# Causal scores on two halves of the PE array's rows, both chains' rotary queries in one step, a new order table, and unused products in three of PE's gaps

## The chip, the cores and the metric

The kernel runs on one core of a Trainium2 chip. Its time is the device time of one execution in microseconds (us); where several executions were timed, the median is given. A profile describes one execution: its *span* runs from the first to the last instruction, and a little time lies around it. The engines are PE (TensorE, matrix products), DVE (VectorE), ACT (ScalarE), POOL (GpSimd) and SP (SyncE, which here only issues transfers, DMAs). PE writes its products to PSUM, in banks of 128 rows by 512 values.

## The reference

One block of a perceiver with a routed feed-forward part, on 256 tokens of width 512, in float32:

```
x = x + cross_attention(layernorm(x), context of 25088 tokens)    # sigmoid scores, no softmax
x = x + causal_attention(layernorm(x))                            # 16 heads of 32, rotary part of 32
x = x + experts(layernorm(x))                                     # argmax over 8 experts, relu(g)^2 * u
```

In the causal attention a score is the sum of two products, one over the 32 values of a head and one over 32 rotary values that all heads share:

```
scores = einsum('bqhd,bkhd->bhqk', q, k) + einsum('bqr,bkr->bqk', q_rope, k_rope)[:, None]
scores = where(causal, -inf, scores / sqrt(HD + D_R))
attn   = einsum('bhqk,bkhd->bqhd', softmax(scores), v) @ W_o
```

## The kernel before

Some 490 us of the span go to the cross attention: 49 pieces of 512 context tokens are loaded, split into high and low parts for products in a faster format, and accumulated in two PSUM banks. Nothing of that is touched.

What follows works on the 256 tokens as two *chains* of 128 tokens, `tt` 0 and 1, which run interleaved. Each piece of work is a *step*, a function such as `Sp(tt, u)`, and the last letter tells its engine: `p` PE, `v` and `w` DVE, `a` ACT, `g` POOL, `s` SP; a step ending in `c` is a copy whose engine is its last argument. The table `ORDER` (line 37) names each step once, with its arguments. The steps are recorded in that order, and `in_order` (line 65) ties each instruction to the one before it on its engine, so each engine works strictly in the order of the table and waits when an input is not there. PSUM banks come from a pool of six (`bank`, line 108) that are handed on when their last reader is done.

The steps of a chain, in order of the data:

- `N1v`, `N1g`, `N1w`, `Xp`, `Xc` (lines 455 to 474): sum, layernorm (the root on POOL), transposition to `xT`.
- `CKp`, `CKc`, `KRp`, `KRv`, `Kp`, `VSp`, `VSc`: compressed keys, rotary keys, keys and values. `Qp` and `QRp`: queries (four steps) and rotary queries. A `prod` is four float32 products over 128 rows.
- `Kc`, `KRc`, `Qc`, `QRc` copy these to the operands of the scores. `kbd` (line 338) is block-diagonal: for each group of four heads it has 128 rows, with keys of one head where its rows are and zeros elsewhere, so that one product with all 128 rows gives two heads. It and the queries `qs` are filled with zeros by POOL first.
- `Sp`, `Sv`, `Sa` (lines 566 to 593): the scores of one unit fill one bank: four heads by 128 keys in chain 0 (4 units), two heads by 256 keys in chain 1 (8 units). A product of the bf16 identity with the mask adds minus infinity above the diagonal. `Sv` takes the maximum, `Sa` the exponential with its sum, one instruction for each head.
- `PTp`, `PTc`, `PVp` (lines 596 to 616): the weights are transposed, copied, and multiplied with the values; each head's result takes 32 rows of PSUM, so heads with different rows can share the PE array.
- `R1v`, `R2p`, `R2c`, `ATv`, `ATa`, `ATw`, `WOp`: division by the sums and output product.
- `N2v`, `N2g`, `N2w`, `Yp`, `Yc` (lines 659 to 684): sum, layernorm and transposition for the experts.
- `LGp`, `LGv`, `RKp`, `RKv`, `RPv` (lines 696 to 750): the choice of expert, counts, and the permutation that sorts tokens into 32-row slots of experts. `RWv` and `RWs` read the numbers of three more experts and load their weights (`mg`, `mh`); `RDs` loads their down weights (`md`).
- `GAp`, `GAc`, `GUp`, `GEa`, `GEv`, `ITp`, `ITc`, `DNp`, `DNa`, `DNv`, `SCp`, `OUv`, `OUs`: sorting, expert products, sorting back, output.

Of the kernel before, what the change touches and what calls it, by code (L numbers as in the profile page):

```python
# [20 lines left out]
P = 128  # L21
# [16 lines left out]
EXa ZSv ZSp O1:0:a AV:0 ZRv O2p:0 AV:1 O2a:0 AV:2 O2v:0 AV:3 Vp:0:0 Vp:0:1 Vp:0:2 Vp:0:3 AV:4 N1v:0 AV:5 AV:6  # L38
AV:7 N1g:0 N1w:0 O1:1:a Xp:0 O2p:1 Xc:0:a O2a:1 CKp:0 O2v:1 Qp:0:0 CKc:0:v Kp:0:0 Kp:0:1 Kc:0:0:3:a Kc:0:0:1:v
Vp:1:0 Kc:0:1:1:a Kc:0:1:3:v Vp:1:1 Vp:1:2 Vp:1:3 VSp:0 WOs N1v:1 Qp:0:1 VSc:0:a Qp:0:2 N1g:1 Qp:0:3 N1w:1 Xp:1  # L40
Qc:0:0:a Qc:0:1:v KRp:0 QRp:0 Xc:1:a KRv:0 QRp:1 KRc:0:1:0:v KRc:0:0:0:a QRv:0 Kc:0:1:2:a CKp:1 Kc:0:0:2:a
KRc:0:0:1:v QRc:0:0:v QRc:0:1:a Qp:1:0 Kc:0:0:0:a QRv:1 CKc:1:a KRc:0:1:1:v Kp:1:0 QRc:1:1:v QRc:1:0:a Kp:1:1
Kc:0:1:0:a Sp:0:1 Sp:0:3 Kc:1:0:3:a Sv:0:1 Sa:0:1 Sp:0:2 Sv:0:3 Kc:1:1:3:v Qp:1:1 Sa:0:3 Kc:1:1:1:v Sv:0:2
Qp:1:2 PTp:0:3 PTp:0:1 Sa:0:2 PTc:0:3:v Qp:1:3 PTc:0:1:v PVp:0:3 Qc:1:0:a Qc:1:1:v PVp:0:1 KRp:1 PTp:0:2 KRv:1
Sp:0:0 PTc:0:2:a KRc:1:1:0:v KRc:1:1:1:v Kc:1:1:2:a VSp:1 KRc:1:0:1:v Kc:1:1:0:a Kc:1:0:1:a Sv:0:0 Sp:1:4
Kc:1:0:0:a VSc:1:a KRc:1:0:0:v Kc:1:0:2:v Sa:0:0 Sp:1:6 Sv:1:4 Sp:1:2 Sv:1:6 Sa:1:4 R1v:0 PTp:0:0 Sp:1:1 Sv:1:2
Sa:1:6 PTc:0:0:v R2p:0 Sv:1:1 PTp:1:6 R2c:0:a Sp:1:7 Sa:1:2 Sp:1:5 Sv:1:7 PTp:1:2 Sv:1:5 Sp:1:3 Sa:1:7 PVp:0:2
Sv:1:3 PVp:0:0 PTc:1:6:a PTp:1:7 ATv:0 PTc:1:2:a PTp:1:4 Sa:1:5 PVp:1:6 PVp:1:2 PTc:1:4:v Sp:1:0 ATa:0 PTc:1:7:v
Sa:1:1 PTp:1:5 ATw:0 PVp:1:4 Sa:1:3 PVp:1:7 Sv:1:0 WOp:0:0 PTc:1:5:v WOp:0:1 PTp:1:3 PTp:1:1 PTc:1:3:a WOp:0:2
# [29 lines left out]
def body(ctx, tc, a, out, nch=NCH):  # L79
# [258 lines left out]
    kbd = [sb.tile([P, 2, 4, T], F32, tag="rT", name=f"kbd{i}", bufs=2) for i in range(2)]  # L338
    for i in range(2):
        nc.gpsimd.memset(kbd[i], 0.0)  # L340
# [14 lines left out]
    trig = sb.tile([64, T], F32, tag="qp0", name="trig")  # L355
    nc.sync.dma_start(trig, a["trig"])
    vs = [sb.tile([P, D], F32, tag=f"kp{i}", name=f"vs{i}", bufs=2) for i in range(2)]
    qs = sb.tile([P, 2, 2, KD, P], F32, tag="N0", name="qs", bufs=2)
    nc.gpsimd.memset(qs, 0.0)
# [140 lines left out]
    @step  # L500
    def QRp(tt):
        ps_["qr", tt] = bank(f"qr_ps{tt}")[0:64, 0:P]
        prod(ps_["qr", tt], tt, lambda j: pw["wqr"][:, 64 * j:64 * (j + 1)])

    @step
    def QRv(tt):
        qr[tt] = sb.tile([32, P], F32, name=f"qr{tt}")
        rotated("q", qr[tt], ps_["qr", tt], tt)

    @step  # L510
    def QRc(tt, i, eng):
        r = 64 - 64 * i
        scaled(eng, qs[r:r + 32, tt, i], qr[tt][:, None, :].broadcast_to([32, KD, P]), 0.125)
# [49 lines left out]
    pr, pt, sc, mx = {}, {}, {}, {}  # L563

    def heads(tt, u):
        return (u, 0, 4) if tt == 0 else (u // 2, 2 * (u % 2), 2)

    @step
    def Sp(tt, u):
        g, h0, n = heads(tt, u)  # L570
        nk = P * (tt + 1)
        p3 = sc[tt, u] = bank(f"s{tt}_{u}").rearrange("p (h k) -> p h k", h=n)
        if tt == 0:
            mm(p3, lhsT=identb, rhs=mask[:, None, :].broadcast_to([P, n, P]), start=True, stop=False)
        for h in range(h0, h0 + n, 2):
            mm(p3[:, h - h0:h - h0 + 2, :], lhsT=qs[:, tt, h // 2, g, :], rhs=kbd[g // 2][:, g % 2, h:h + 2, :nk],  # L576
               start=tt == 1, stop=tt == 0 and h == 2)
        if tt == 1:
            mm(p3[:, :, P:], lhsT=identb, rhs=mask[:, None, :].broadcast_to([P, n, P]), start=False, stop=True)

    @step
    def Sv(tt, u):
        mx[tt, u] = sm.tile([P, 4], F32, tag="mx", name=f"mx{tt}_{u}", bufs=4)
        nc.vector.tensor_reduce(mx[tt, u][:, :heads(tt, u)[2]], sc[tt, u], AX.X, ALU.max, negate=True)

    @step
    def Sa(tt, u):
        g, h0, n = heads(tt, u)
# [353 lines left out]
```

## Time and profile before

| What | us |
|---|---|
| median of three runs | 581.35 (580.42 to 581.46) |
| the profiled execution | 580.47 |
| its span | 578.50 |
| last product of the cross attention ends | 490.4 |
| first scores of the causal attention (chain 0) start | 507.32 |
| output product of chain 0 complete, `N2v` starts | 535.40 |
| transposition for the experts, chain 0, starts (`Yp:0`) | 539.56 |
| the same for chain 1 (`Yp:1`) | 546.23 |
| first expert product starts (`GUp:0:0:0`) | 553.08 |
| last product ends | 574.76 |

How to read such numbers: the share of busy time is an average, and matmul ends are modelled, so a full PE row does not tell that PE could not go faster. The granted clock tells how fast the array was allowed to run; it is shown in the row PEclk and in each stretch of a table by stage. In listings of instructions, "128*32" is the part of the array used (rows by columns), "128x256" the result's shape, and a float32 product shows as two records. A bracket at the end of a row tells how long the engine was idle before it and what ended that.

### The profile page before, as it was taken

Reading aid. Unit: us, or ns where it says so; the run is one execution under the profiler, and the core shown is the slowest. Engines: PE = TensorE matmul, PEld = TensorE weight load, DVE = VectorE, ACT = ScalarE, POOL = GpSimd, SP = SyncE. Lnnn points to the kernel's source line nnn. Section 1 sums busy time; section 2 is a strip of 40 time slices with the busy share of each in tenths; the row PEclk is TensorE's granted clock in tenths of the full one; section 3 lists DMA queues with packets and bytes.
Section 4 is the critical chain, followed back from the end, with each engine's and each line's share of the span. In section 5 each row is a group of like instructions: output and inputs, shape, how many; then the busy total and the mean of one; then the engine's idle time right before and its main releaser. Section 6 shows DMA issues by size and latency. Waiting matters only on the chain.

```text
span 578.5 us, 7915 instructions
## 1 busy us (share of the span) xinstructions
PE 560.4 (97%) x3044; PEld 465.3 (80%) x3044; DVE 447.3 (77%) x513; ACT 388.0 (67%) x497; POOL 22.5 (4%) x36
## 2 busy tenths in 40 slices
PE   4999999999999999999999999999999999999697
PEld 3888888888888888888888888888888887876563
DVE  5899888878787878787878787878787865575754
ACT  5877777777777777777777777777777763376332
POOL 5200000000000000000000000000000023000000
PEclk9999999999999999999999999999999999999889
DMA  8897878876575656565657575756465554300081
GB/s 285 347 368 277 288 278 304 304 257 254 183 251 187 255 180 253 187 247 188 248 190 252 181 254 184 256 181 255 180 257 181 213 193 175 146 2 1 5 306 56
DMA packets 22725, 124.49 MB, mean 215 GB/s; under 512 B 3040, under 2 KB 3232, under 8 KB 9376
## 3 DMA queue, kind: packets, MB, share of 16 engines
q1 hardware_dynamic: 22688, 123.99, 59.4%
q8 instruction: 24, 0.39, 0.3%
q14 instruction: 13, 0.11, 0.1%
HBM read 121.36 MB, written 2.62 MB: 214 GB/s over the span
## 4 chain that ended last, share of the span: by engine, by line
PE 94%; DVE 3%; issue 1%; ACT 1%; DMA 1%; POOL 0%; SPq 0%; DVEq 0%; ACTq 0%; POOLq 0%
PE acc L98 15%; PE acc L99 15%; PE acc L100 15%; PE kp_ps L99 8%; PE kp_ps L98 8%; PE kp_ps L100 8%; PE sc L100 4%; PE sc L99 4%; PE sc L98 4%; PE s L576 2%; PE gu L813 2%; PE q_ps L479 1%; PE pt L600 1%; PE dn L842 1%; PE pv L615 1%
## 5 line engine op out<-in xcount | busy, mean ns | idle before, releaser
L95 DVE TENSOR_TENSOR N<-rN,N 128x2048 fp32r<-128x2048 f32 (+1 forms) x53 | 111.8, 2114 | 57.7 <-ACT N L94 57.6
L98 PE MATMUL acc<-N,z 128*128 128x512 f32 x392 | 153.9, 393 | 0.0
L99 PE MATMUL acc<-N,z 128*128 128x512 f32 x392 | 153.7, 392 | 0.0
L100 PE MATMUL acc<-N,z 128*128 128x512 f32 x392 | 152.5, 389 | 0.0
L95 DVE TENSOR_TENSOR T<-rT,T 128x2048 fp32r<-128x2048 f32 (+1 forms) x49 | 110.3, 2253 | 17.2 <-ACT T L94 17.2
L220 ACT ACTIVATE z<-sc 128x512 f32<-128x512 f32 x98 | 58.7, 599 | 78.8 <-PE sc L100 78.6
L94 ACT CAST N<-rN 128x2048 fp32r<-128x2048 f32 (+1 forms) x55 | 94.4, 1725 | 6.1
L94 ACT CAST T<-rT 128x2048 fp32r<-128x2048 f32 (+1 forms) x55 | 94.1, 1717 | 0.1
L100 PEld LDWEIGHTS acc<-N,z 128*128 128x128 f32 x392 | 73.6, 188 | 16.1
L98 PEld LDWEIGHTS acc<-N,z 128*128 128x128 f32 x392 | 74.0, 189 | 12.3
L99 PEld LDWEIGHTS acc<-N,z 128*128 128x128 f32 x392 | 74.0, 189 | 11.6
L98 PE MATMUL kp_ps<-T,wk 128*128 128x512 f32 x196 | 76.9, 392 | 0.0
L100 PE MATMUL kp_ps<-T,wk 128*128 128x512 f32 x196 | 76.7, 391 | 0.0
L99 PE MATMUL kp_ps<-T,wk 128*128 128x512 f32 x192 | 74.7, 389 | 0.0
L222 DVE TENSOR_TENSOR zacc<-zacc,z 128x512 f32<-128x512 f32 x98 | 67.5, 688 | 7.0 <-ACT z L220 1.5
L95 DVE TENSOR_TENSOR z<-z,z 128x512 fp32r<-128x512 f32 x98 | 67.5, 689 | 0.0
L94 ACT CAST z<-z 128x512 fp32r<-128x512 f32 x98 | 61.0, 623 | 3.1
L211 ACT ACTIVATE kp<-kp_ps,bk 128x512 fp32r<-128x512 f32 x49 | 33.9, 691 | 39.9 <-PE kp_ps L100 39.9
L100 PE MATMUL sc<-qp,kp 128*128 128x256 f32 x196 | 55.8, 285 | 0.1
L99 PE MATMUL sc<-qp,kp 128*128 128x256 f32 x196 | 55.4, 283 | 0.0
L98 PE MATMUL sc<-qp,kp 128*128 128x256 f32 x196 | 54.9, 280 | 0.0
L98 PEld LDWEIGHTS kp_ps<-T,wk 128*128 128x128 f32 x196 | 37.1, 189 | 7.8
(209 smaller groups left out, 561.8 us busy)
## 6 DMA issues: line engine op xcount, KB each, us to landing
rN<-in_ctxN SPq DMA_DIRECT2D x49, 1024.0 KB, 4.8
rT<-in_ctxT SPq DMA_DIRECT2D x47, 1024.0 KB, 4.9
gu<-in_gu SPq DMA_DIRECT2D x4, 1024.0 KB, 7.2
sp_wo<-w_wo SPq DMA_DIRECT2D x8, 256.0 KB, 4.0
wo<-sp_wo SPq DMA_DIRECT2D x2, 1024.0 KB, 6.0
mg<-in_gu SPq DMA_DIRECT2D x4, 512.0 KB, 4.0
md<-in_dn SPq DMA_DIRECT2D x6, 256.0 KB, 7.2
rT<-in_ctxT SPq DMA_DIRECT2D x4, 256.0 KB, 6.1
```

Source lines behind the costliest of these rows:

```text
L94: copy(hi, src)
L95: eng.tensor_tensor(lo, src, f(hi), ALU.subtract)
L98: mm(ps, lhsT=ahi, rhs=bhi, start=first, stop=False)
L99: mm(ps, lhsT=ahi, rhs=blo, start=False, stop=False)
L100: mm(ps, lhsT=alo, rhs=bhi, start=False, stop=last)
L211: nc.scalar.activation(kp[c][0], ps, AF.Identity, bias=bk)
L220: nc.scalar.activation(z, ps, AF.Sigmoid, scale=1.0 / math.sqrt(128.0))
L222: tt2(zacc, zacc, z, ALU.add)
L479: mm(ps, lhsT=w(j), rhs=xT[tt][:, j, :], start=j == 0, stop=j == KD - 1)
L576: mm(p3[:, h - h0:h - h0 + 2, :], lhsT=qs[:, tt, h // 2, g, :], rhs=kbd[g // 2][:, g % 2, h:h + 2, :nk], start=tt == 1, stop=tt == 0 and h ...
L600: nc.tensor.transpose(ps[:, toks(i * (tt + 1) + kt)], pr[tt, u][:, i, toks(kt)], ident)
L813: mm(gps[tt, g][r, :], lhsT=yg[tt][:, j, at], rhs=w[:, 2 * j * P:2 * (j + 1) * P], start=j == 0, stop=j == KD - 1)
```

## The change

Scores. `kbd` is replaced by `ks`, and `qs` is laid out alike: head h of a group sits, with its 32 rows of data and 32 rows of rotary data, in rows 0 to 63 (h 0 and 1) or 64 to 127 (h 2 and 3). A score is a product over 64 rows, on the upper or the lower half of the array's rows. `Sp(tt, k)` makes two units at a time, one in each half and each in its own bank, with their products alternating. The memsets go. The copies change: `Kc` is 4 copies of 32x512 a chain (before, 8 of 32x256), `KRc` 4 of 32x512 (as before), `Qc` 4 of 32x512 (before, 2 of 64x512), `QRc` 4 of 32x512 (before, 2).

Rotary queries. `QRp` makes both chains at once, on the two halves of the array's columns; `trig` is loaded twice, for rows 0 to 63 and 64 to 127, with two DMAs.

Values. `PVp(tt, k)` takes two units at a time, so in chain 1 four heads with four different row blocks follow each other (before, two). Chain 1's weights and their transposes have four buffers each instead of two, and the maxima have eight.

`N1s` and `N2s` are parts of `N1v` and `N2v` with a name of their own. `WMp(n, k)` multiplies the identity with the mask k times into a bank that nobody reads: 7, 9 and 2 times at three places.

The order table is new from `N1v` on. The lines around the causal attention, and those with `WMp`, are shown; the rest of the table is cut.

```diff
 ORDER = """
...
-Kc:0:1:0:a Sp:0:1 Sp:0:3 Kc:1:0:3:a Sv:0:1 Sa:0:1 Sp:0:2 Sv:0:3 Kc:1:1:3:v Qp:1:1 Sa:0:3 Kc:1:1:1:v Sv:0:2
...
+AV:6 AV:7 N1g:0 N1w:0 O1:1:a Xp:0 O2p:1 Xc:0:a O2a:1 CKp:0 O2v:1 Qp:0:0 CKc:0:a Vp:1:0 Vp:1:1 Vp:1:2 Vp:1:3 Kp:0
+WOs N1v:1 Qp:0:1 N1s:1 Kc:0:0:a Kc:0:3:a Qp:0:2 N1g:1 Kc:0:1:a Qp:0:3 N1w:1 Kc:0:2:a Xp:1 Qc:0:1:a VSp:0 Xc:1:v
+Qc:0:2:a Qc:0:0:a KRp:0 VSc:0:v QRp Qc:0:3:a KRv:0 KRc:0:0:v KRc:0:2:a KRc:0:1:v Qp:1:0 KRc:0:3:v QRv:0 Qp:1:1
+QRc:0:1:v QRc:0:0:a QRv:1 Qp:1:2 QRc:0:2:a QRc:0:3:v QRc:1:0:v QRc:1:1:a Qp:1:3 QRc:1:2:v QRc:1:3:a Sp:0:1
+Qc:1:2:a Qc:1:1:a Qc:1:3:a CKp:1 Sv:0:2 Qc:1:0:a Sv:0:3 Sa:0:2 Sp:0:0 CKc:1:v KRp:1 Sa:0:3 Sv:0:1 Kp:1 KRv:1
+VSp:1 Kc:1:1:a Sv:0:0 Kc:1:3:a PTp:0:3 KRc:1:2:v KRc:1:0:v PTp:0:2 Kc:1:2:a KRc:1:1:v KRc:1:3:v Kc:1:0:a
+PTc:0:2:v Sa:0:1 PTc:0:3:v Sp:1:1 VSc:1:v Sa:0:0 PVp:0:1 Sv:1:3 PTp:0:1 Sv:1:2 Sa:1:3 Sp:1:0 PTc:0:1:v R1v:0
+PTp:0:0 Sa:1:2 Sv:1:0 PTp:1:3 R2p:0 PTc:0:0:a Sv:1:1 PTp:1:2 Sa:1:0 PTc:1:3:v PVp:0:0 PTc:1:2:v Sp:1:3 Sa:1:1
+R2c:0:v PTp:1:0 ATv:0 PTp:1:1 PTc:1:0:a Sv:1:6 PVp:1:1 PTc:1:1:a Sv:1:7 Sp:1:2 ATa:0 Sa:1:7 ATw:0 PVp:1:0 Sv:1:4
+Sa:1:6 WOp:0:0 Sv:1:5 PTp:1:7 Sa:1:4 PTp:1:6 PTc:1:7:v WOp:0:1 Sa:1:5 PTc:1:6:v PTp:1:4 WOp:0:2 PTc:1:4:a R1v:1
+WOp:0:3 PTp:1:5 N2v:0 R2p:1 PTc:1:5:a N2s:0 PVp:1:3 R2c:1:a PVp:1:2 N2g:0 ATv:1 N2w:0 ATa:1 Ya:0 ATw:1 WMp:0:7
+Yp:0 Yv:0 Yc:0:a WOp:1:0 WOp:1:1 WOp:1:2 WOp:1:3 LGp:0 N2v:1 N2s:1 LGv:0 N2g:1 N2w:1 WMp:1:9 RKp:0 RKv:0 Yp:1
+Ya:1 RPv:0 Yc:1:a WMp:2:2 LGp:1 RWv:0 GAp:0:0 LGv:1 GAp:0:3 RWs:0 GAc:0:0:a PMp:0 GAc:0:3:a GAp:0:1 Yv:1 RKp:1
+PMc:0:a GAp:0:2 RKv:1 GAc:0:1:a GUp:0:0:0 GAc:0:2:a RPv:1 GUp:0:1:0 GUp:0:0:1 GUp:0:0:2 GUp:0:0:3 RWv:1
+GUp:0:1:1 GEa:0:0 RWs:1 GUp:0:1:2 GEv:0:0 GUp:0:1:3 GAp:1:2 GEa:0:1 GAp:1:1 GEv:0:1 GAc:1:2:a PMp:1 GAc:1:1:a
+GAp:1:3 PMc:1:v ITp:0:1 GAp:1:0 GAc:1:3:a ITc:0:1:v ITp:0:0 GUp:0:2:0 GAc:1:0:a ITc:0:0:v GUp:0:2:1 GUp:1:0:0
...
-    kbd = [sb.tile([P, 2, 4, T], F32, tag="rT", name=f"kbd{i}", bufs=2) for i in range(2)]
-    for i in range(2):
-        nc.gpsimd.memset(kbd[i], 0.0)
+    ks = sb.tile([P, 2, KD, T], F32, tag="rT", name="ks", bufs=2)
...
+    trig = sb.tile([P, T], F32, tag="qp0", name="trig")
+    for i in range(2):
+        nc.sync.dma_start(trig[64 * i:64 * i + 64], a["trig"])
...
     @step
-    def QRp(tt):
-        ps_["qr", tt] = bank(f"qr_ps{tt}")[0:64, 0:P]
-        prod(ps_["qr", tt], tt, lambda j: pw["wqr"][:, 64 * j:64 * (j + 1)])
+    def QRp():
+
+        ps_["qr"] = bank("qr_ps")[:, 0:P]
+        for j in range(KD):
+            for t in range(2):
+                mm(ps_["qr"][64 * t:64 * t + 64], lhsT=pw["wqr"][:, 64 * j:64 * (j + 1)], rhs=xT[t][:, j, :],
+                   start=j == 0, stop=j == KD - 1)
...
+    sides = [(e, 64 * i + 32 * e, 64 * i + 32 - 32 * e) for e in range(2) for i in range(2)]
...
+    def Kc(tt, i, eng):
+        e, r, _ = sides[i]
+        cp[eng](ks[r:r + 32, e, :, toks(tt)], ps_["k", tt][r:r + 32])
...
+        e, r, _ = sides[i]
+        scaled(eng, qs[r:r + 32, tt, e], ps_["q", tt][r:r + 32], 0.125)
...
+        k, i = divmod(u, 2)
+        return [4 * g + 2 * i + e for g in ((2 * k, 2 * k + 1) if tt == 0 else (k,)) for e in range(2)]
...
+    def Sp(tt, k):
         nk = P * (tt + 1)
+        hs = [heads(tt, 2 * k + i) for i in range(2)]
+        n = len(hs[0])
+        p3 = [bank(f"s{tt}_{2 * k + i}").rearrange("p (h k) -> p h k", h=n) for i in range(2)]
+        masks = mask[:, None, :].broadcast_to([P, n, P])
         if tt == 0:
+            for i in range(2):
+                mm(p3[i], lhsT=identb, rhs=masks, start=True, stop=False)
+        for j in range(n):
+            for i in range(2):
+                g, h = divmod(hs[i][j], 4)
+                r = slice(64 * i, 64 * i + 64)
+                mm(p3[i][:, j, :], lhsT=qs[r, tt, h % 2, g, :], rhs=ks[r, h % 2, g, :nk],
+                   start=tt == 1 and j == 0, stop=tt == 0 and j == n - 1)
         if tt == 1:
+            for i in range(2):
+                mm(p3[i][:, :, P:], lhsT=identb, rhs=masks, start=False, stop=True)
...
+    def PVp(tt, k):
...
+        units = (2 * k, 2 * k + 1)
+        n = len(heads(tt, 2 * k))
         for kt in range(tt + 1):
+            for j in range(0, n, 2):
+                for u in units:
+                    for i in (j, j + 1):
+                        g, h = divmod(heads(tt, u)[i], 4)
+                        r = slice(32 * h, 32 * h + 32)
+                        mm(pv[tt][r, g, :], lhsT=vs[kt][:, g * P + r.start:g * P + r.stop],
+                           rhs=pt[tt, u][:, toks(i * (tt + 1) + kt)], start=kt == 0, stop=kt == tt)
...
+    def WMp(n, k):
+
+        ps = bank(f"idle{n}")
+        for _ in range(k):
+            mm(ps, lhsT=identb, rhs=mask[:, None, :].broadcast_to([P, 4, P]), start=True, stop=True)
```

## The prediction

> **What bounds the kernel now.** First the page's busy times, then a table by stage, since the average is made by the 490 us that the change leaves alone.
>
> ```profile
> PE 560.4 (97%) x3044; PEld 465.3 (80%) x3044; DVE 447.3 (77%) x513; ACT 388.0 (67%) x497; POOL 22.5 (4%) x36
> ```
>
> The table by stage has, for each stretch, its length, then the busy time of each engine, the granted clock and the DMA share.
>
> ```profile
> 507.30:512.00 4.70, 4.70 (x30) 4.12 (x29) 3.08 (x6) 3.55 (x19) 0.00 (x0) 1.00 0.02 3
> 517.00:522.00 5.00, 5.00 (x20) 2.34 (x19) 4.81 (x12) 4.60 (x20) 0.00 (x0) 1.00 0.00 0
> 527.00:532.00 5.00, 5.00 (x51) 3.43 (x50) 3.82 (x7) 4.14 (x15) 0.00 (x0) 1.00 0.01 3
> 537.00:540.00 3.00, 1.39 (x22) 1.15 (x21) 1.98 (x5) 1.93 (x4) 0.55 (x1) 1.00 0.00 0
> 540.00:545.00 5.00, 3.73 (x22) 3.16 (x21) 2.67 (x8) 0.66 (x2) 0.05 (x1) 1.00 0.00 0
> 545.00:550.00 5.00, 3.29 (x16) 2.83 (x16) 4.02 (x19) 1.20 (x2) 0.50 (x1) 0.59 0.13 22
> 550.00:555.00 5.00, 5.00 (x49) 3.71 (x51) 3.41 (x17) 1.44 (x3) 0.00 (x0) 0.73 0.78 297
> ```
>
> In the causal attention (507 to 537) PE has no pause, but ACT and DVE are at 60 to 95%: PE work taken out pays until ACT becomes the bound. From 537 to 550 PE waits for layernorm and routing on DVE, and the clock falls: in finer stretches it is 0.50 from 545.9 to 552.7, that is 6.8 us. Third, PE's listing for single steps (start, duration, pause before it):
>
> ```profile
> 502.02 1.91 PE L479 MATMUL qr_ps<-xT,wqr 128*64 128x128 f32 x16
> 514.20 0.64 PE L615 MATMUL pv<-pt,vs 128*32 128x128 f32 x16
> 517.57 1.02 PE L576 MATMUL s<-kbd,qs 128*128 128x512 f32 x2
> 527.91 1.07 PE L615 MATMUL pv<-pt,vs 128*32 128x128 f32 x16
> 539.56 0.63 PE L172 MATMUL xc_ps<-ident,xc 128*128 128x128 f32 x4 [1.61 <-DVE xc L167]
> 542.78 0.95 PE L699 MATMUL lg_ps<-gate,yT 128*128 128x8 f32 x8
> 545.65 0.17 PE L715 MATMUL rk_ps<-hot,before 128*128 128x8 bf16 x1 [1.92 <-DVE hot L710]
> 547.99 1.88 PE L699 MATMUL lg_ps<-gate,yT 128*128 128x8 f32 x8 [0.68 <-ACT yT L684]
> ```
>
> The two `lg` rows are the same work at full and at half clock. Two `pv` rows of 16 records differ: four heads side by side take 0.57 on the chain of waits, two side by side 1.00. Last, ACT and DVE, back to back:
>
> ```profile
> 520.27 0.47 ACT L592 ACTIVATE pr<-s,mx 128x256 f32<-128x256 f32 x1 [0.18 <-DVE mx L584]
> 521.19 0.47 ACT L592 ACTIVATE pr<-s,mx 128x256 f32<-128x256 f32 x1
> 526.68 1.07 ACT L605 COPY pt<-pt 128x512 f32<-128x512 f32 x2 [0.28 <-PE pv L615]
> 519.49 1.29 DVE L584 TENSOR_REDUCE mx<-s 128x2 f32<-128x512 f32 x2
> ```
>
> So a chain-1 `Sa` (two heads) costs ACT 0.92; a chain-0 `Sa` (four heads, starts 509.32 and 510.71) 1.39; a 512-wide copy about 0.50 on ACT and 0.60 on DVE.
>
> **PE work taken out.** *Scores:* the chain of waits gives 0.86 for one unit's float32 products in either chain (517.73 on), 12 units, 10.3. Two halves at once give 0.86 for two units, 6 steps, 5.2: saved 5.2. *Rotary queries:* 16 records in 1.91 become 16 in about 0.9 on two column halves: saved 0.9. *Values:* chain 1 pays four times 1.00 for two units; with four heads side by side 0.57: saved 1.7 to 2.0. Together some 8, but this is PE time, not span.
>
> A rule speaks against the first item. The Trainium skill, "TensorE: Matmul & The Clock Gate", section "LDWEIGHTS (loading the stationary operand)", says that a weight load takes its columns divided by 1.2 per ns, however few rows: 107 ns for 128 columns, also on half the rows. The `lg` row agrees (0.95/8 = 119 ns a record, with only 8 columns streaming). Chain 0's new products have 128 moving columns, and before, one load served 256. If the two halves' loads queue, chain 0's step costs 16 x 0.107 = 1.7 and not 0.86, and nothing is saved there; chain 1 has 8 x 0.107 = 0.86 beside 0.86 of products. "TensorEngine Tiling (Array Packing)", "Key Properties", has tiles loading in parallel, but the array drained when the tiling changes. No row here is row-tiled. For drains the `pv` row is nearest: 0.57 where 2 x 0.213 were pure, so 0.14 for entry and exit. I take chain 0 between its ends, 1.3, and 0.14 for each visit.
>
> **What the other engines make of it.** I laid the new table out by hand, each step at the latest of its engine, its inputs and its bank. Up to `Qp:0:0` (494.03) nothing moves. Then chain 1's value products come ahead of `Kp:0` (start of `N1v:1` 497.08, before 497.89), `Qp` 0:1 to 0:3 run to 500.44, `Xp:1` follows, `Xc:1` on DVE ends 501.77. From there DVE leads: `VSc` 0.72, `KRv` with one `KRc` 1.36, two `KRc` 0.88, `QRv` 0.92, `QRc` 0.44, `QRv` 0.81, `QRc` 0.42, to 507.5. PE, done with all of `Qp:1` at 506.45, waits a us; the first scores are complete at 508.3. So here nothing is won, but three `Qp` are already behind.
>
> From then ACT leads, nearly without a pause: four `Qc:1` to 510.3; `Sa` 0:2 and 0:3 to 513.05; four `Kc:1` to 515.1 (these hold `Sp:1:1` back: PE waits 1.1 us); `Sa` 0:1 and 0:0 to 517.8; `Sa` 1:3, 1:2 to 519.65; `PTc:0:0` and `Sa` 1:0, 1:1 to 522.05; then 0.8 of waiting for `PTp:1:0`, which stands behind `Sp:1:3` (held until `Sa:1:0` frees one of its banks at 521.1; ends 522.25); two `PTc` and `ATa:0` to 524.5; `Sa` 1:7, 1:6, 1:4, 1:5 to 528.2. PE follows: `WOp:0` to 529.65 (before 535.3), `PTp:1:5`, `R2p:1`, `PVp` 1:3 and 1:2 to 531.7, DVE's `ATv:1` and `N2w:0` to 533.1, `Yp:0` at 533.15 instead of 539.56: 6.4 won. PE's own work from 508.3 to 531.7 is 21.1 of 23.4, so ACT leaves it 2.3 of waits, where it had none. Chain 0's slower loads (0.44 a step) are mostly behind ACT: 0.3. Drains: 6 x 0.14, half of them where PE is waited for: 0.3. **Won here: 5.8.**
>
> *Costed at nothing:* the second `trig` DMA (0.56 of SP's queue at 478, behind it only the `wo` loads at 497.6; needed at 502.7; uncovered it would cost its 0.56); the memsets that go (POOL's next work, the root, waits for DVE at 489.4 in any case); the split of `N1v` and `N2v` (order on DVE unchanged).
>
> **The tail.** `WMp`: a bf16 product of 512 columns takes 0.213 (the masks at 507.32 and 507.53). `WMp:0` 7 x 0.213 = 1.5 fits in the pause of 1.61 ahead of `Yp:0`, `WMp:1` 9 x 0.213 = 1.92 in that of 1.92 ahead of `RKp:0`, `WMp:2` 0.43 in `Yp:1`'s wait for ACT's copy. Queued behind them are just those steps, which wait for DVE; I expect at most 0.1. What they can bring is the clock. At half speed before were: `Yp:1` 1.09 instead of 0.60, `LGp:1` 1.88 instead of 0.95, `PMp:0` 0.73 instead of 0.33, six `yg` records 1.92 instead of 1.2, 0.15 more to 552.7: 2.7. Since `RPv:0` now comes ahead of `RWv:0`, the permutation is ready 0.6 earlier and doesn't take this back (`perm:0` 541.95, `LGp:1` ends 542.05). `GUp:0:0:0` then starts at 544.1, 9.0 ahead of 553.08. From there to the last product before, 21.7 us, PE had no pause, and the work is the same.
>
> The rule: the page on TensorE, Part 1 ("HAM oscillation"), has the clock halved by PE gaps longer than some 3.4 us, the window in which activity is judged. Here the fall at 545.9 came after 542.8, from when PE had only the 0.95 of `lg` and 0.2 of `rk`, and lasted 6.83 us. The new worst 3.4 us (`RKp:0` to `GAp:0:0`) hold 1.5 of dense work and 0.95 of `lg`. By the gap rule the clock stays: 2.6. By the row alone it is open, as no window here lies between a tenth and two thirds: 0 to 2.6. I take it as held, less 0.2 for expert weights: their numbers come 4.6 earlier (542.55), the DMA 1.1 later as before, and 1.5 MB took 5.7 from issue, so they land at 549.4; `GUp:0:2:0` wants them at 549.9. Half a us of slack. **Won here: 2.4.**
>
> Sum against the profiled execution: 580.47 (span 578.50 and 1.97 around it) less 8.2 is 572.3. The median lies 0.88 above that execution; I keep the difference: **573.2**.
>
> **Rivals.**
> - *The clock falls all the same in the routing stage.* For it: `lg` and transpositions may hardly count as activity. Against: 11 products in the holes. The 2.6 stay lost: 575.8.
> - *The row halves don't overlap.* Each score step costs 1.71. `Sp:1:1` then ends at 518.1 (laid out: 516.25), `Sp:1:3` 3.1 and `Sp:1:2` 4.0 later, the last `Sa` 3.2 later: 3.5 on the end, less the 0.3 for loads already counted: 576.4. For it: no row shows them; against: columns of the array do overlap (`pv`, 0.57).
> - *Slower: the clock falls inside the attention,* since PE now waits for ACT there. 511.7 to 515.2 holds only 1.8 of PE work, half transpositions. A window at half speed loses 1.7 of work; five of the seven windows from 508 to 533 outweigh 8.2, and all seven, less some 2 of PE's slack, give about 583. Against it: at half speed PE would be full again, and before, the clock came back after dense work.
> - *The change doesn't do what it says:* `WMp` cannot fill anything if DVE is earlier than laid out; then it delays by the overlap, at most 3.8 in all. Its pauses depend on unchanged DVE steps, so it has no own share.
>
> **How the numbers follow.** Forecast 0.60 (its own range 570.8 to 574.8); clock 0.14; halves 0.14; better than laid out, under 570.8, 0.05; no change 0.02; slower 0.05. Faster than 0.2% (1.2 us, about what can be told from no change here): 0.93. The range reaches from 570.8 to 577.6, past the clock and halves cases with their own us of error; some 0.15 lie outside.
>
> **What would show it.** `Yp:0` near 533.7, `GUp:0:0:0` near 544.9, records of `s` on 64 rows starting in pairs, 0.86 a score step, `pv` of chain 1 0.57, clock 1.00 throughout, ACT above 90% busy from 508 to 528, no wait for `mg`. Wrong if a score step takes 1.7, if 0.50 shows in the clock, or if `WMp` ends after its successor's input.

## The result and the profile after

The changed kernel takes 574.35 us (median of four, 573.70 to 574.78) where the kernel before takes 580.89 (580.42 to 581.46) on the same chip: a ratio of 0.9886, with a 95% interval of 0.9869 to 0.9903. The forecast was 573.2, in a range of 570.8 to 577.6. The profiled execution took 573.7, its span 571.8; before, the span was 578.5. So 6.7 us of span went, 0.1 of it in the cross attention, where the prediction's sum had 8.2.

The last product of the cross attention, which nothing here touches, ends between 489.8 and 491.5 in the profiles of this study. So the tail is measured from that end, in three stretches: **A** to the first transposition for the experts (`Yp:0`), **B** from there to the first expert product, **C** from there to the end of the last product.

| us | before | forecast | after | won, forecast | won, measured |
|---|---|---|---|---|---|
| A | 49.17 | 43.3 | 44.36 | 5.8 | 4.8 |
| B | 13.51 | 11.1 | 10.93 | 2.4 (2.6 less 0.2) | 2.6 |
| C | 21.69 | 21.7 | 22.54 | 0 | -0.85 |

First the page of the changed kernel: its span, the row of the granted clock in 40 slices, and the sums.

```profile
span 571.8 us, 8000 instructions
...
PE 556.8 (97%) x3094; PEld 461.2 (81%) x3094; DVE 446.8 (78%) x512; ACT 390.4 (68%) x498; POOL 17.3 (3%) x33
...
PEclk9999999999999999999999999999999999999999
```

As before, the sums say little: PE is 97% busy in both. The table by stage tells more. Its columns are the length of the stretch, the busy time of PE, PE's weight loads, DVE, ACT and POOL, the granted clock, the DMA share and GB/s.

```profile
507.30:512.00 4.70, 4.70 (x51) 3.85 (x50) 3.39 (x8) 4.64 (x15) 0.00 (x0) 1.00 0.00 0
517.00:522.00 5.00, 5.00 (x66) 3.81 (x64) 4.79 (x9) 5.00 (x24) 0.00 (x0) 1.00 0.00 0
...
537.00:540.00 3.00, 3.00 (x20) 2.13 (x19) 1.82 (x6) 0.00 (x0) 0.00 (x0) 1.00 0.00 0
540.00:545.00 5.00, 4.41 (x30) 3.08 (x29) 4.51 (x22) 2.07 (x5) 0.55 (x1) 1.00 0.00 0
545.00:550.00 5.00, 5.00 (x74) 3.10 (x74) 3.51 (x18) 1.90 (x6) 0.00 (x0) 1.00 0.83 280
550.00:555.00 5.00, 5.00 (x61) 3.12 (x63) 1.52 (x5) 2.19 (x5) 0.00 (x0) 1.00 0.96 322
```

Two things are new. The clock is 1.00 in every row (it falls again at 569.8, after the last product), where before it was 0.59 and 0.73 from 545 to 555. And from 517 to 522 PE and ACT are both full. Which of the two leads is told by the chain of waits (start, duration, what), not by this table:

```profile
515.06 0.58 ACT ks L546
515.68 1.13 PE s L593 x8
516.82 0.33 PE s L597 x2
517.14 0.57 PE pv L639 x16
...
523.40 0.87 PE pt L620 x8
524.27 0.57 PE pv L639 x16
...
531.97 1.01 PE pv L639 x32
532.98 1.63 PE idle L894 x7
534.61 0.63 PE xc_ps L171 x4
```

From the first scores of chain 1 (515.68) to the unused products (532.98) there is not one ACT or DVE step in it: 17.3 us of PE alone. Ahead of that it is ACT's, with four copies `ks` from 513.29 on. PE's listing shows the steps that changed.

```profile
507.06 1.20 PE L593 MATMUL s<-ks,qs 64*128 64x128 f32 x16
515.68 1.13 PE L593 MATMUL s<-ks,qs 64*128 64x256 f32 x8 [1.27 <-ACT ks L546]
516.75 0.39 PE L597 MATMUL s<-mask,identb 128*128 128x256 bf16 x2
517.07 0.65 PE L639 MATMUL pv<-pt,vs 128*32 128x128 f32 x16
...
538.65 2.10 PE L894 MATMUL idle<-mask,identb 128*128 128x512 bf16 x9
...
542.59 1.06 PE L726 MATMUL lg_ps<-gate,yT 128*128 128x8 f32 x8 [0.24 <-ACT yT L711]
...
556.89 0.40 PE L840 MATMUL gu<-mh,yg 128*32 128x256 f32 x1 [0.21 <-DMA mh<-in_gu]
```

The `s` rows run on 64 rows of the array; a chain-1 step of two units lasts from 515.68 to 517.07 with its masks, 1.39, where two units were 1.94 in the chain of waits before (0.86 and 0.11 each). A chain-0 step of 16 records takes 1.13 to the next step at 508.19. `lg` of chain 1 takes 1.06 and not 1.88. The last row is a wait that the prediction did not have.

Inside the step at 515.68 the single records of the trace show how the halves run (start in us, duration in ns; the two columns are the two halves; only the second load of each half is shown):

```
product       515.685           515.691
weight load   515.791  186      515.798  186
product       516.005           516.011
product       516.221           516.227
product       516.436           516.443
mask          516.751           516.871
```

Loads and products of the halves go 6 to 7 ns apart, a pair every 0.2155 us. From the first pair to the second it is 0.32, from the last pair to the mask 0.31.

### The profile page after: what moved, and what is told of

Read it like the earlier page. It is cut to its first block, busy times and chain, and to the rows that moved or that the text cites. A ratio compares the mean times of both kernels' runs of the same rounds, so it can differ in the third digit from the quotient of the medians.

```text
span 571.8 us, 8000 instructions
## 1 busy us (share of the span) xinstructions
PE 556.8 (97%) x3094; PEld 461.2 (81%) x3094; DVE 446.8 (78%) x512; ACT 390.4 (68%) x498; POOL 17.3 (3%) x33
```

## The experiments

**1. Unused products, one at each place instead of 7, 9 and 2.**

```diff
-WOp:0:3 PTp:1:5 N2v:0 R2p:1 PTc:1:5:a N2s:0 PVp:1:3 R2c:1:a PVp:1:2 N2g:0 ATv:1 N2w:0 ATa:1 Ya:0 ATw:1 WMp:0:7
-Yp:0 Yv:0 Yc:0:a WOp:1:0 WOp:1:1 WOp:1:2 WOp:1:3 LGp:0 N2v:1 N2s:1 LGv:0 N2g:1 N2w:1 WMp:1:9 RKp:0 RKv:0 Yp:1
-Ya:1 RPv:0 Yc:1:a WMp:2:2 LGp:1 RWv:0 GAp:0:0 LGv:1 GAp:0:3 RWs:0 GAc:0:0:a PMp:0 GAc:0:3:a GAp:0:1 Yv:1 RKp:1
+WOp:0:3 PTp:1:5 N2v:0 R2p:1 PTc:1:5:a N2s:0 PVp:1:3 R2c:1:a PVp:1:2 N2g:0 ATv:1 N2w:0 ATa:1 Ya:0 ATw:1 WMp:0:1
+Yp:0 Yv:0 Yc:0:a WOp:1:0 WOp:1:1 WOp:1:2 WOp:1:3 LGp:0 N2v:1 N2s:1 LGv:0 N2g:1 N2w:1 WMp:1:1 RKp:0 RKv:0 Yp:1
+Ya:1 RPv:0 Yc:1:a WMp:2:1 LGp:1 RWv:0 GAp:0:0 LGv:1 GAp:0:3 RWs:0 GAc:0:0:a PMp:0 GAc:0:3:a GAp:0:1 Yv:1 RKp:1
```

> The changed kernel with one unused product at each of the three places instead of 7, 9 and 2 (a product each stays so that the PSUM banks are handed on as before). Theory, the products hold the clock: 0.50 shows for 6.8 us from 537 to 542 on, the way from the transposition for the experts to the first expert product grows from 10.9 to some 13.4 us, and the time is 576.8. Rival one, the shorter routing holds it alone: clock 1.00, 574.3. Rival two, the products only delay their successors: clock 1.00, 574.1 or less.

Measured: 576.05, ratio 0.9920 (0.9903 to 0.9936). A is unchanged (44.36), B is 12.49 instead of 10.93. The table by stage of this kernel:

```profile
540.00:545.00 5.00, 2.46 (x18) 1.77 (x17) 4.50 (x22) 1.21 (x2) 0.55 (x1) 0.99 0.00 0
545.00:550.00 5.00, 5.00 (x45) 3.57 (x48) 3.40 (x17) 2.40 (x5) 0.00 (x0) 0.67 0.59 191
```

The clock shows 0.50 from 544.89 for 3.41 us, half the 6.83 of the kernel before. PE's busy time in the five us ahead is 2.46, against 4.41 with the products. So the products hold the clock, and that is worth 1.56 of B in this profile. Two things go with the number. C is 21.71 here and not 22.54: over the three stretches the products win 0.7 only, since an earlier start of the expert products costs 0.8 behind it (why, is told with the tail below), and 1.3 of the 2.0 between the two spans lies in the cross attention. And the profiled execution may show too little: its mean clock is 0.996, that of the three others 0.993 and 0.994, as in the kernel before (0.992 to 0.994), so the clock was probably low for longer in them.

**2. The products alone, in the kernel before.** `WMp` is added to the old table, ahead of `Yp:0`, `RKp:0` and `LGp:1`; nothing else changes.

```diff
-ATa:1 N2w:0 Ya:0 ATw:1 Yp:0 Yv:0 Yc:0:a WOp:1:0 WOp:1:1 WOp:1:2 WOp:1:3 LGp:0 N2v:1 LGv:0 N2g:1 RKp:0 N2w:1
-RKv:0 Yp:1 Ya:1 RWv:0 Yc:1:a RPv:0 RWs:0 LGp:1 Yv:1 PMp:0 GAp:0:0 LGv:1 PMc:0:a GAp:0:1 GAc:0:0:v GAp:0:2
+ATa:1 N2w:0 Ya:0 ATw:1 WMp:0:7 Yp:0 Yv:0 Yc:0:a WOp:1:0 WOp:1:1 WOp:1:2 WOp:1:3 LGp:0 N2v:1 LGv:0 N2g:1 WMp:1:9 RKp:0 N2w:1
+RKv:0 Yp:1 Ya:1 RWv:0 Yc:1:a RPv:0 RWs:0 WMp:2:2 LGp:1 Yv:1 PMp:0 GAp:0:0 LGv:1 PMc:0:a GAp:0:1 GAc:0:0:v GAp:0:2
```

> The kernel before with the unused products alone, 7 ahead of the transposition for the experts of chain 0, 9 ahead of the count step, 2 ahead of the second expert choice. Theory, the clock was what the routing stage lost: clock 1.00, the way from that transposition to the first expert product goes from 13.5 to 10.9 us, 578.2. Rival, the order of the routing steps on DVE takes part of it back (the permutation is 0.6 later than in the changed kernel): 11.5 us, 578.9. Rival two, no gain: 580.9.

Measured: 578.67, ratio 0.9963 (0.9949 to 0.9977). A and C stay (49.07, 21.71); B goes from 13.51 to 11.37, with the clock at 1.00. Of B's 2.6 us some 2.1 are thus the products. The other 0.44 (11.37 less 10.93) is what the new order around the routing is worth at full clock; the permutation ahead of the expert numbers is probably the main part of it, but had no run of its own.

**3. Only the nine products ahead of the count step.** `WMp:1:9` stays as it is.

```diff
-WOp:0:3 PTp:1:5 N2v:0 R2p:1 PTc:1:5:a N2s:0 PVp:1:3 R2c:1:a PVp:1:2 N2g:0 ATv:1 N2w:0 ATa:1 Ya:0 ATw:1 WMp:0:7
-Ya:1 RPv:0 Yc:1:a WMp:2:2 LGp:1 RWv:0 GAp:0:0 LGv:1 GAp:0:3 RWs:0 GAc:0:0:a PMp:0 GAc:0:3:a GAp:0:1 Yv:1 RKp:1
+WOp:0:3 PTp:1:5 N2v:0 R2p:1 PTc:1:5:a N2s:0 PVp:1:3 R2c:1:a PVp:1:2 N2g:0 ATv:1 N2w:0 ATa:1 Ya:0 ATw:1 WMp:0:1
+Ya:1 RPv:0 Yc:1:a WMp:2:1 LGp:1 RWv:0 GAp:0:0 LGv:1 GAp:0:3 RWs:0 GAc:0:0:a PMp:0 GAc:0:3:a GAp:0:1 Yv:1 RKp:1
```

> The changed kernel with one product instead of seven ahead of Yp:0 and one instead of two ahead of LGp:1; the nine ahead of the count step stay. If the nine alone hold the clock through the routing, the stretch from Yp:0 to the first expert product stays 10.9 us, the clock shows 1.00 throughout and the time is 574.4. If all three places are needed, the clock falls to 0.50 for about 3.4 us, the stretch is 12.5 and the time 576.0.

Measured: 573.91, ratio 0.9884 (0.9868 to 0.9901). B is 10.94, and the table by stage has:

```profile
540.00:545.00 5.00, 4.20 (x30) 3.04 (x28) 4.51 (x22) 2.18 (x5) 0.45 (x1) 1.00 0.00 0
545.00:550.00 5.00, 5.00 (x75) 3.10 (x73) 3.50 (x18) 1.89 (x6) 0.00 (x0) 1.00 0.83 293
```

Nine products in one pause are enough, with one left at each of the other two places; more there brings nothing. It costs nothing either: A is 44.34 with one product ahead of `Yp:0` and 44.36 with seven.

**4. The two units of a step one after the other,** each with its mask beside its own products.

```diff
-        if tt == 0:
-            for i in range(2):
+        for i in range(2):
+            if tt == 0:
...
-        for j in range(n):
-            for i in range(2):
+            for j in range(n):
...
-        if tt == 1:
-            for i in range(2):
+            if tt == 1:
```

> The changed kernel with each unit's mask next to its own products, so that a product with the whole array stands between the two halves in the queue and they cannot run at once. A score step should take some 2.0 us in chain 1 with its masks instead of 1.28, and some 2.1 in chain 0. Theory by the layout on record, 3.5 on the end: 577.9. Rival, ACT hides most: 1.5 on the end, 575.9. Rival two, nothing of the halves matters: 574.4.

Measured: 579.97 (579.51 to 585.53 in twelve executions), ratio 0.9995 (0.9972 to 1.0017): the whole gain is gone. PE's listing of this kernel:

```profile
517.30 1.13 PE L592 MATMUL s<-ks,qs 64*128 64x256 f32 x4 [0.70 <-DVE ks L535]
518.36 0.28 PE L595 MATMUL s<-mask,identb 128*128 128x256 bf16 x1
518.57 1.13 PE L592 MATMUL s<-ks,qs 64*128 64x256 f32 x4
519.63 0.28 PE L595 MATMUL s<-mask,identb 128*128 128x256 bf16 x1
519.84 0.65 PE L637 MATMUL pv<-pt,vs 128*32 128x128 f32 x16
```

A step takes 2.54 instead of 1.39, 1.15 more; six steps make 6.9, and A is 6.03 longer (50.39). Where the missing 0.9 stays, the starts tell: `Sp:1:1` begins 26.83 after the cross attention instead of 25.42, so the two steps of chain 0, 2.3 of PE time, cost 1.4 there, and the four of chain 1, 4.6 of PE time, cost 4.6 behind it. Up to `Sp:1:1` ACT and DVE hide part of what PE does; from there on nothing hides it. A single unit on half the rows is also dearer than it was on all rows, 1.27 against 0.97, since every unit now pays for the changes of the tiling that two shared.

**5. Halves in turn, masks together.** The loop over halves goes outside the loop over heads.

```diff
-        for j in range(n):
-            for i in range(2):
+        for i in range(2):
+            for j in range(n):
```

> The changed kernel with all products of one half of the rows first and then those of the other, so that neighbours in the queue use the same half. Theory, the halves run at once and that counts on the path: a score step of chain 1 goes from 1.07 to some 1.8 us, and the end moves by 3.2: 577.5. Rival, ACT leads in the attention and hides what PE does: the step takes 1.8 as well, but the time is 575 or less. If the step stays at 1.07, the order in the queue doesn't matter.

Measured: 575.06, ratio 0.9902 (0.9885 to 0.9919); A is 45.25, 0.89 longer. The listing:

```profile
506.96 1.71 PE L593 MATMUL s<-ks,qs 64*128 64x128 f32 x16
...
515.71 1.90 PE L593 MATMUL s<-ks,qs 64*128 64x256 f32 x8 [0.70 <-DVE ks L535]
...
519.02 1.14 PE L593 MATMUL s<-ks,qs 64*128 64x256 f32 x8
```

Chain 0's steps (1.64 to the next step, with 8 records a half) and the first of chain 1 (1.83) lose part or all of the overlap, but the other three of chain 1 (4 records a half) lose nothing: their records still start in pairs, at 519.341 and 519.354, 519.556 and 519.570, although in the order of the code three records of the first half lie ahead of the second half's first. In chain 0 the second half's first record starts behind the fifth of eight (507.507 and 507.513): there, too, three are left. So alternating in the code is needed for the longer steps. The first step of chain 1 runs in turn for another reason: the second half's first weight load, the one with a wait, starts at 516.476, just after DVE's first copy `pt` has ended (515.73 and 0.69), which by the table frees its bank. In the changed kernel that copy ends at 515.48, ahead of the step. So 0.76 of the 0.89 is this wait, and the 1.0 of PE time that chain 0's steps lose costs 0.1, since PE waits there for ACT and DVE in any case (`Sp:1:1` starts 25.53 after the cross attention instead of 25.42).

**6. Values of chain 1 unit by unit,** as the kernel before had them.

```diff
-        for kt in range(tt + 1):
+        for half in ((units,) if tt == 0 else ((units[0],), (units[1],))):
+          for kt in range(tt + 1):
...
-                for u in units:
+                for u in half:
```

> The changed kernel with chain 1's value products unit by unit, two heads side by side as before. Each of the four steps takes 1.0 instead of 0.57. Theory, only those behind which the layernorm waits count, two at the end of the attention and one ahead of the output product: 1.0 more, 575.4. Rival one, all four on the path: 1.7 more, 576.1. Rival two, hidden: 574.4.

Measured: 574.63, ratio 0.9887 (0.9866 to 0.9907); A is 44.39, and a `pv` step shows 0.66 for 0.64. The order of the heads inside a step is worth nothing; what counts is that the two units use four different column blocks. In the chain of waits of before, the two pairs of units that took 1.00 used the same two blocks twice (`PVp:1:6` and `1:2`, `1:5` and `1:3`), and a pair with four different blocks (`1:4` and `1:7`) took 0.59 already:

```profile
527.98 1.00 PE pv L615 x16
...
530.58 0.59 PE pv L615 x16
...
535.00 1.00 PE pv L615 x16
```

The last pair (`1:1` and `1:0`, 0.99 in PE's listing) had four blocks too, but its second unit started only at 537.316, when ACT's copy of its weights was done.

**7. One of ACT's copies ahead of `Sp:1:1` to DVE.**

```diff
-Qc:1:2:a Qc:1:1:a Qc:1:3:a CKp:1 Sv:0:2 Qc:1:0:a Sv:0:3 Sa:0:2 Sp:0:0 CKc:1:v KRp:1 Sa:0:3 Sv:0:1 Kp:1 KRv:1
+Qc:1:2:a Qc:1:1:a Qc:1:3:a CKp:1 Sv:0:2 Sv:0:3 Sa:0:2 Sp:0:0 CKc:1:v Qc:1:0:v KRp:1 Sa:0:3 Sv:0:1 Kp:1 KRv:1
```

> The changed kernel with one of the four copies of chain 1's queries, the last, on DVE instead of ACT, after the copy of the compressed keys, where DVE has a pause of 1.2 us. Theory, ACT leads the attention and each of its copies on 32 rows costs 0.585: the stretch from the end of the cross attention to the transposition for the experts goes from 44.4 to 43.8. Rival, what ACT gives up DVE takes: the first scores of chain 1 also wait for DVE's copy of the transposed weights (515.5): 0.2 at most.

Measured: 574.69, ratio 0.9886 (0.9870 to 0.9903). `Sp:1:1` starts 24.98 after the cross attention instead of 25.42, so 0.44 of the copy's 0.59 is won there (one reason for the rest stands with the next experiment), but A falls by 0.18 only:

```profile
516.47 1.40 PE L593 MATMUL s<-ks,qs 64*128 64x256 f32 x8 [0.87 <-ACT ks L546]
```

The step itself now takes 1.33 to its masks at 517.80 instead of 1.07: the load of its second half waits until 516.735, and DVE's first copy `pt`, which by the table frees its bank, ends at 516.68. So 0.26 of what was won at the head is lost at once.

**8. What a copy costs on ACT.** Chain 0's copies of keys and queries alternate between their two banks. The copy of chain 1's queries that the expectation gives to DVE stays on ACT in this table; the copies compared here are chain 0's.

```diff
-WOs N1v:1 Qp:0:1 N1s:1 Kc:0:0:a Kc:0:3:a Qp:0:2 N1g:1 Kc:0:1:a Qp:0:3 N1w:1 Kc:0:2:a Xp:1 Qc:0:1:a VSp:0 Xc:1:v
-Qc:0:2:a Qc:0:0:a KRp:0 VSc:0:v QRp Qc:0:3:a KRv:0 KRc:0:0:v KRc:0:2:a KRc:0:1:v Qp:1:0 KRc:0:3:v QRv:0 Qp:1:1
+WOs N1v:1 Qp:0:1 N1s:1 Qp:0:2 N1g:1 Qp:0:3 N1w:1 Xp:1 Kc:0:0:a Qc:0:1:a Kc:0:3:a VSp:0 Xc:1:v
+Qc:0:2:a Kc:0:1:a Qc:0:0:a KRp:0 VSc:0:v QRp Kc:0:2:a Qc:0:3:a KRv:0 KRc:0:0:v KRc:0:2:a KRc:0:1:v Qp:1:0 KRc:0:3:v QRv:0 Qp:1:1
```

> Chain 0's copies of keys and queries on ScalarE alternate between the two banks (one of keys, one of queries), where the changed kernel does four of one bank in a row; one copy of chain 1's queries goes to VectorE. If successive copies overlap as soon as they read different banks, one takes 0.48 to 0.50 us where they follow back to back; if a copy of 32 rows by 512 costs 0.585 anyway, 0.585 stays. Since the copies come later and chain 1's queries wait for their banks, the time is 0 to 1.5 us above the changed kernel.

Measured: 574.35 in one execution, A 44.34. ACT's listing of this kernel, and then of the changed kernel:

```profile
500.82 0.59 ACT L377 ACTIVATE qs<-q_ps 32x512 f32<-32x512 f32 x1 [2.10 <-PE q_ps L479]
501.42 0.58 ACT L546 COPY ks<-k_ps 32x512 f32<-32x512 f32 x1
502.01 0.59 ACT L377 ACTIVATE qs<-q_ps 32x512 f32<-32x512 f32 x1
```

```profile
513.29 2.34 ACT L546 COPY ks<-k_ps 32x512 f32<-32x512 f32 x4
523.88 1.07 ACT L625 COPY ptb<-pt 128x512 f32<-128x512 f32 x2 [1.29 <-PE pt L620]
```

Copies of 32 rows start 0.59 (`ks`) or 0.60 (`qs`) apart, from alternating banks as from one, while two copies of 128 rows take 1.07, so that the second starts 0.48 after the first. The bank is not the reason. Nor is it the number of rows alone, as ACT's listings of the kernel before, and then of the run with one copy on DVE, tell:

```profile
504.38 0.63 ACT L539 COPY kbd<-k_ps 32x256 f32<-32x256 f32 x2
...
507.45 0.75 ACT L539 COPY kbd<-k_ps 32x256 f32<-32x256 f32 x2
```

```profile
509.33 1.79 ACT L377 ACTIVATE qs<-q_ps 32x512 f32<-32x512 f32 x3
511.14 0.37 ACT L612 ACTIVATE pr<-s,mx 128x128 f32<-128x128 f32 x1
```

By the table, the two copies at 504.38 have the same rows (64 to 95): the second starts 0.27 after the first and overlaps its end by 0.09. Those at 507.45 have different rows (96 and 0 on): 0.385, no overlap. And `Sa` starts 0.49 after a `qs` copy of rows 0 to 31 (changed kernel, 509.93) but 0.61 after one of rows 96 to 127 (with one copy on DVE, 510.53). In all pairs of this attention that follow each other back to back and read PSUM, the second overlaps the first by some 0.1 where both begin at the same row, and not at all where they begin at different rows; a copy of 128 rows with one of rows 64 on behind it (515.83 in the kernel before) has no overlap either. Copies from SBUF show no overlap in either case. No run was made to test this, and why it is so is open. In the changed kernel and in this experiment alike, each copy of a group begins at another row than the one ahead of it.

**9. Chain 1's expert numbers ahead of its permutation.**

```diff
-PMc:0:a GAp:0:2 RKv:1 GAc:0:1:a GUp:0:0:0 GAc:0:2:a RPv:1 GUp:0:1:0 GUp:0:0:1 GUp:0:0:2 GUp:0:0:3 RWv:1
-GUp:0:1:1 GEa:0:0 RWs:1 GUp:0:1:2 GEv:0:0 GUp:0:1:3 GAp:1:2 GEa:0:1 GAp:1:1 GEv:0:1 GAc:1:2:a PMp:1 GAc:1:1:a
+PMc:0:a GAp:0:2 RKv:1 RWv:1 RWs:1 GAc:0:1:a GUp:0:0:0 GAc:0:2:a RPv:1 GUp:0:1:0 GUp:0:0:1 GUp:0:0:2 GUp:0:0:3
+GUp:0:1:1 GEa:0:0 GUp:0:1:2 GEv:0:0 GUp:0:1:3 GAp:1:2 GEa:0:1 GAp:1:1 GEv:0:1 GAc:1:2:a PMp:1 GAc:1:1:a
```

> The changed kernel with chain 1's reading of the expert numbers and the DMA for their weights ahead of its permutation, so that the DMA goes out some 1.6 us earlier. Theory, the last 0.85 us is a wait for expert weights: the stretch from the first expert product to the last product goes from 22.5 to 21.7, the time from 574.35 to 573.5. Rival, the DMA engines are full from 547 to 560 and the weights come no earlier: 22.5 as before. Rival two, the later permutation makes PE wait ahead of chain 1's sorting: 22.5 or more.

Measured: 573.89, ratio 0.9870 (0.9854 to 0.9887); C is 22.20 instead of 22.54, which alone says little, since an unchanged tail came out at 22.09 as well (experiment 11).

**10. Both edits, and two transposition steps ahead of `Sp:1:3`.** The two edits just shown, and:

```diff
-PTp:0:0 Sa:1:2 Sv:1:0 PTp:1:3 R2p:0 PTc:0:0:a Sv:1:1 PTp:1:2 Sa:1:0 PTc:1:3:v PVp:0:0 PTc:1:2:v Sp:1:3 Sa:1:1
-R2c:0:v PTp:1:0 ATv:0 PTp:1:1 PTc:1:0:a Sv:1:6 PVp:1:1 PTc:1:1:a Sv:1:7 Sp:1:2 ATa:0 Sa:1:7 ATw:0 PVp:1:0 Sv:1:4
+PTp:0:0 Sa:1:2 Sv:1:0 PTp:1:3 R2p:0 PTc:0:0:a Sv:1:1 PTp:1:2 Sa:1:0 PTc:1:3:v PVp:0:0 PTc:1:2:v Sa:1:1
+R2c:0:v PTp:1:0 ATv:0 PTp:1:1 Sp:1:3 PTc:1:0:a Sv:1:6 PVp:1:1 PTc:1:1:a Sv:1:7 Sp:1:2 ATa:0 Sa:1:7 ATw:0 PVp:1:0 Sv:1:4
```

> The copy on DVE and the numbers first, and also chain 1's first two transpositions of weights ahead of the third score step, for which ACT waits 1.3 us. Theory, the parts add: the stretch to the transposition for the experts 43.5, that from the first expert product to the last product 21.7, the time 572.9. Rival, the later score step costs what ACT wins: 573.3.

Measured: 573.53, ratio 0.9870 (0.9854 to 0.9887). C is 21.80; A is 44.37, so the moved transpositions give back the 0.18 of the copy. The wait of 0.8 for them that the prediction had laid out was not on the path that sets the end.

**11. The two edits without the third, and the changed kernel once more** beside it on the same chip.

> The changed kernel with both edits that paid a little: one copy of chain 1's queries on VectorE, and chain 1's expert numbers read ahead of its permutation. If the two add up: 44.2 us from the cross attention to Yp:0 and 22.2 from the first expert product to the last, together 0.5 less than the changed kernel, 573.7. If they do not, no difference from the changed kernel, 574.3.

> The changed kernel once more, unchanged, beside the version with both edits, to compare the two on one chip: 574.3, a ratio of 0.9886 to the kernel before. A difference of 0.1 per cent from the version with both edits is about what five rounds can tell.

Measured: 573.02 (572.38 to 573.05), ratio 0.9869 (0.9853 to 0.9885), against 573.82 (572.97 to 574.02), ratio 0.9884 (0.9867 to 0.9900), four executions each. SP's queue (start, time to issue) for the second set of weights in the version with both edits, and in the changed kernel of this run:

```profile
546.76 0.86 SPq L788 DMA_DIRECT2D mg<-in_gu  x2
547.86 0.33 SPq L788 DMA_DIRECT2D mh<-in_gu  x1
```

```profile
548.56 0.86 SPq L788 DMA_DIRECT2D mg<-in_gu  x2
549.66 0.33 SPq L788 DMA_DIRECT2D mh<-in_gu  x1
```

It is asked for 1.8 us after the first expert product starts (544.92) instead of 3.3 after (545.24), and C is 21.82 instead of 22.09. In the seven profiles that keep the changed order there and the products at their places, C lies between 22.09 and 22.77; in two of the three with the numbers first it is 21.80 and 21.82, nearly as before the change, in the third 22.20. The medians are 0.8 apart and the profiled spans 0.59; of the latter 0.27 is C and 0.13 is A (44.20 against 44.33), and the rest lies in the cross attention, which no edit touches. The version with both edits is the fastest of the study by its median, but the intervals of the two ratios overlap.

## Why the prediction was right, and where it was off

**Row halves: right, and the risk did not come.** The step taken for chain 0 was 1.3, between 0.86 and 1.7, from the rule on weight loads of the Trainium skill ("TensorE: Matmul & The Clock Gate", section "LDWEIGHTS (loading the stationary operand)"). Measured is 1.13: the two halves' loads start 7 ns apart, so they do not queue, as "TensorEngine Tiling (Array Packing)", "Key Properties", has it.

**The saving of the scores was mis-sized.** The sum had 5.2 less small terms for drains: "0.14 for each visit", half of them covered (that half is 0.42, of which the sum took 0.3). A chain-1 step takes 1.39, of which 0.86 is products and 0.22 masks, so a visit costs 0.31: some 0.1 between the first two pairs (0.32 from start to start instead of 0.2155), 0.1 ahead of the mask (0.31), 0.1 ahead of `pv`; behind transpositions there is another 0.1 ahead of the first pair. The row the 0.14 was taken from, a `pv` step, holds only one such change. What was saved is then 4 x (1.94 - 1.39) in chain 1 and 2 x (2.16 - 1.66) in chain 0 (masks included, from the listings' starts), 3.2 in all.

**"From then ACT leads, nearly without a pause": right up to `Sp:1:1`, wrong from there on.** ACT is busy 93% of 508 to 528, as the prediction wanted to see (18.61 of 20.00). Up to 515.68 it sets the pace (1.0 of PE time added to chain 0 in experiment 5 moved `Sp:1:1` by 0.1). Behind that PE does: the chain of waits is PE alone, PE waits nowhere in those 17.3 us, ACT has pauses of 1.29 ahead of 523.88 and 0.67 ahead of 529.79. With the units apart, 4.6 of PE time added in this part cost 4.6, and 6.03 of 6.9 over the whole of A, where the rival "the row halves don't overlap" let 3.5 of some 5 through, with ACT as cover. The laid-out PE work had been too short by the drains above. That `PVp` still ends when it was laid out (17.30 from `Sp:1:1`, against 17.15 with loads and drains) is luck, one error against another: 1.2 us of waits for ACT that did not occur, and about as much of tiling changes that did.

**"A 512-wide copy about 0.50 on ACT": the term behind most of A's miss.** It was read from copies of 128 rows that begin at the same row (1.07 for two). The eight copies ahead of `Sp:1:1` have 32 rows, each beginning at another row than the one before, and their two groups take 2.30 (from 508.13) and 2.35 (from 513.29) where 2.0 and 2.05 were laid out. That is 0.6 of the 0.69 by which `Sp:1:1` is late (25.42 after the cross attention, laid out 24.73); two `Sa` between them are the other 0.1. A misses by 1.0; the remaining 0.3 are the 0.15 above and 0.15 ahead of `Yp:0`. The page of before had a warning row: its `qs` copies of 32 by 512 from SBUF took 0.63.

**"Chain 1 pays four times 1.00": three times,** as the kernel before shows (1.00, 0.59, 1.00, 0.99), so 1.3 was to be had and not 1.7 to 2.0.

**The clock: right in size.** It is at 1.00 throughout, B is 10.93, and 2.1 of the 2.6 come with the products alone; the trace of before, in which the cost of the fall was added up step by step, gave 2.7 for it. Which of them is needed was not asked: nine in one pause. The gap rule that the prediction cites gave the right answer for the changed kernel, but read as it stands it would have kept the clock in the kernel before as well: PE's longest pause ahead of that fall was 1.92 (to 545.65), and 1.79 ahead of the one with a single product at each place (to 542.06), both well under 3.4. So the fall does not need one long pause; a stretch with little PE work is enough. How little was not measured here. The rivals "the clock falls all the same" and "inside the attention" are out: no stretch below 1.00 before the last product, but for the first 13 us of the span.

**The tail: "from there 21.7 to the last product", "no wait for `mg`": the second set of weights was left out.** The first set was priced with 0.2, from a slack that was misread: "1.5 MB took 5.7 from issue", while in the trace of before both sets took 6.5 from the first issue to the last landing (548.32 to 554.79). In the changed kernel the first set takes 6.8, and its `mh` lands at 551.68, 0.4 after PE could have used it, which does not move the end. But the new order puts chain 1's numbers (`RWv:1`) behind its permutation and the first expert products, and their transfers (548.87 on SP) then run beside those of chain 0 and the down weights: the DMA engines are 0.83 to 0.96 busy from 545 to 555. The second set is asked for 3.3 us after the first expert product starts, where it was 2.1, and takes 8.0 where it took 6.5. PE stands still for its `mh` at 556.89.

All of C's 0.85 is this wait. The records of the traces tell when the second `mh` lands, when the first product with it starts, and C (us after the first expert product starts):

| kernel | `mh` landed | first product with it | C |
|---|---|---|---|
| one unused product each (1) | 9.15 | 10.52 | 21.70 |
| both edits and transpositions (10) | 10.55 | 10.60 | 21.80 |
| both edits (11) | 10.58 | 10.62 | 21.82 |
| changed, once more (11) | 10.85 | 10.90 | 22.09 |
| numbers first (9) | 10.96 | 11.00 | 22.20 |
| changed | 11.29 | 11.34 | 22.54 |
| banks in turn (8) | 11.56 | 11.60 | 22.77 |

Where `mh` is there in time, the product starts at 10.52 and C is 21.70; elsewhere the product starts 0.04 to 0.05 after the landing, and C is longer by as much as it is late, to 0.02 us, in all twelve profiles with the new order. The list of PE's waits shows it only in part (0.21 at 556.89, none in the kernel once more), because products on other column blocks run meanwhile.

## What to carry to other kernels

A copy's cost is to be taken from a row of the same shape and with the same neighbour: fewer rows did not make it cheaper, and the error came eight times over on one queue. Two engines that are both full look alike in a table of busy times; which one leads is read from the chain of waits, and a forecast that rests on "the other engine hides it" should be tried by adding work to the hidden one. When a stage starts earlier, every transfer that it waits for must land earlier too, the second set as well as the first; asking for it 1.5 us earlier brought its last part in at 10.55 to 10.96 instead of 10.85 to 11.56, with the DMA engines this full. And a wait on one part of the array does not show as a pause of PE: look at the first product with the tile, beside its landing.

## What the hardware showed that was not expected

- Products on the two halves of the array's rows, with their weight loads, run fully side by side: 6 to 7 ns apart, a pair every 0.2155 us. Going between half rows and the whole array, or to column blocks, costs about 0.1 us each time.
- PE starts products of the other half ahead of the order in which the code has them (6 to 14 ns after one of the first half), as soon as three of the first half are left, in steps of four and of eight alike; chain 0's steps then need 1.64 instead of 1.13.
- Copies of 32 rows by 512 on ACT, each beginning at another row, start 0.59 to 0.60 apart, those of 128 rows 0.48; of 32 rows by 256, the one pair with the same rows starts 0.27 apart, those with different rows 0.38.
- Nine bf16 products of 512 columns (2 us in all) in one pause keep the clock at 1.00 through 5 us of otherwise thin work; without them it falls for one stretch of 3.41 us or, before, one of 6.83.
